# A four-layer convolutional block on one core: earlier loads into the expert layer, a later gate check and fewer PSUM turns

## The chip, the cores and the metric

The kernel runs on one core of one Trainium2 chip. All data are 32-bit floats. The metric is the device time of one execution, in microseconds (us); "before" below is the median of three executions. PE is the matrix engine, DVE the vector engine, ACT the scalar engine, POOL the GpSimd engine, and SP the engine that does little but issue transfers.

## The reference

The input has 8 images of 384 channels and 32 x 32 pixels. Four layers follow one another, each as a residual on a group norm of 32 groups:

```python
x = x + attention(_gn(x))   # layer 0: q, k, v = pw @ gelu(bn(depthwise3x3(x))); softmax(q k) v per head
                            #          (8 heads); w_out; bn over the batch
x = x + experts(_gn(x))     # layer 1: 4 experts, w2 @ relu(w1 @ x + b1) + b2, summed with coefficients
x = x + conv7(_gn(x))       # layer 2: depthwise 7x7, reflected edges
x = x + branches(_gn(x))    # layer 3: three branches; gelu(mw1 x) mw2 on two quarters of the channels,
                            #          depthwise kxk on the others (k = 1, 3, 5), fused with weights
                            #          that come from the branches' means; final projection
```

In layer 1 the gate gives each token its two best experts. The coefficient of an expert depends on whether the expert is chosen by any token at all in first place, and in second place (`present`). Since all four are normally chosen in both places, the kernel computes the coefficients as if that were so, checks afterwards that it was, and computes layers 1 to 3 again if not. That branch isn't taken with these inputs.

## The kernel before, in words

**Order and buffers.** PE, ACT and DVE keep the order in which the program issues their instructions (`manual_schedule(engines=ORDERED)`); in layers 2 and 3 POOL does too. SP issues only transfers, in one queue[...]. Buffers come from pools. A tile of a pool opened with `reuse_waits="tile"` waits only for the last users of the very memory that it overlaps; in other pools the first use waits for everything that lay in the pool's memory before.

**Layer 0.** Depthwise convolutions are matmuls with band matrices (L467). Projections of q and k (L613) and v (L668), scores (L715), exponentials on ACT (L722), values (L734) and the output projection (L790) follow; its result z goes to DRAM from POOL's queue. While the last image is computed, x of each image is read again for statistics (SP).

**From layer 0 to layer 1.** The batch norm of z gives a scale `zn_s` and a shift `zn_t` (`bn_coefs`; the power -1/2 is on POOL). The group norm of layer 1 is worked out from moments of z and x without a pass over their sum: a chain of small DVE operations, a matmul that sums over the groups (gn_ps, L264), `from_moments`, with the powers on POOL (s, L290). `experts()` then opens its pools. `residual(b)` loads z and x in three parts each (L1096, L1097) and adds them on DVE (L1103) to r; `normed` makes xn from r on ACT.

**Layer 1.** For each image b and half h, `TODO` runs over 12 pairs of expert and third of the hidden channels: matmuls ph (L1267), relu on ACT. DVE forms sums of the hidden tiles (`HSUMS`, L1161), POOL has formed sums of weights (`WSUMS`, L1147, 13 operations), and the products p (L1168) of these are added to r on DVE (L1182, L1184). While image b + 1 runs, the generator `next_layer(b)` (called `passing` in the loop) takes image b on to layer 2: statistics, group norm, then for each third of the channels ACT xn (`pass_on`), a transpose on DVE (L957) and a store. The loop calls it after the hidden tiles k = 0, 2, 3, 4, 6 and 8. `logits(b)` (called `gating`) computes the gate, for the last image also the check: ranks of the experts per token, whether any token chose each (anyp), a matmul with ones (pp, L1028), and the flag `repeat`.

**Layer 2.** `convolve7` (L1045) runs over groups of channels. xt are the transposed images, loaded by SP (L1583) for the second and third group. Weights w come through `load_weights` (L1450), are combined at two edges on POOL, and spread by ACT (wx, L1471). Finished groups are evicted from PSUM by ACT (o, L352).

**Layer 3.** `convolve3` (L1716) works as layer 2 does. Two PSUM buffers of four banks each take turns:

```python
def four_banks(turn=True):
    ps = tps[len(taken) % 2].tile([P, 4, HF], FP, tag="ps", name="ps")
    if turn:
        taken.append(1)
    return ps
```

`banks(turn)` cuts small pieces from such a buffer. With `turn=False` the next caller gets the same buffer. A group of convolutions is 160 matmuls, and after the first 80 of some groups `hidden3(i)` (L1916) computes the hidden channels of two images in a buffer of its own. `branch_mean` (L1948), `branch_weights` (L1971) and the bias pb (L1824) are small matmuls in such buffers too. A POOL queue of transfers reorders y in DRAM meanwhile (ya<-y), and SP loads it. The final projection (L2128) follows.

Of the kernel before, what the change touches and what calls it, by code (L numbers as in the profile page):

```python
# [18 lines left out]
P = 128  # L19
# [117 lines left out]
def conv_mixer_kernel(ctx: ExitStack, tc: tile.TileContext, a: dict, out: bass.AP):  # L137
# [13 lines left out]

    parity = const.tile([P, 2], FP, name="parity")
# [122 lines left out]
    def from_moments(own, ps, ref, s, t, gm, firsts=None):  # L275

        c, n = ps.shape[1], ps.shape[3]
        both, sq = (
            own.tile([P, c, n], FP, tag=f"fm_{k}", name=f"fm_{k}") for k in "ab"
        )  # L280
        nc.vector.tensor_copy(both, ps[:, :, 0])
        nc.vector.tensor_mul(sq, both, both)
        nc.vector.scalar_tensor_tensor(
            out=sq, in0=ps[:, :, 1], scalar=EPS, in1=sq, op0=ALU.add, op1=ALU.subtract
        )
        nc.vector.tensor_add(gm, both, ref)
        for n0, n1 in firsts or ((0, n),):
            shape = [P, c, n1 - n0]
            half = mhalf[:, 0:1].unsqueeze(2).to_broadcast(shape)
            nc.gpsimd.tensor_tensor(  # L290
                out=s[:, :, n0:n1], in0=sq[:, :, n0:n1], in1=half, op=ALU.pow
            )
            nc.vector.scalar_tensor_tensor(
                out=t[:, :, n0:n1], in0=gm[:, :, n0:n1], scalar=-1.0, in1=s[:, :, n0:n1],
                op0=ALU.mult, op1=ALU.mult,
            )
# [13 lines left out]
    def bn_coefs(stats, gb, n, s, t):  # L310

        mv = small.tile([P, 2, 9], FP, tag="bn_mv", name="bn_mv")
        for i in range(n):
            nc.vector.bn_aggr(mv[:, :, i], stats[:, i].rearrange("p a s -> p (a s)"))
        rsqrt(s, mv[:, 1, :n])
        nc.vector.tensor_mul(s, s, gb[:, :, 0])
        nc.vector.tensor_mul(t, mv[:, 0, :n], s)
        nc.vector.tensor_sub(t, gb[:, :, 1], t)
# [18 lines left out]
    mv3 = const.tile([P, 2, NC, B], FP, name="mv3")  # L337

# [19 lines left out]
    with (  # L358
# [6 lines left out]
        bn_gb = load(cw, "bn_gb", nc.scalar)  # L365
        stats = cw.tile([P, 9, 2 * B, 6], FP, name="stats")
# [11 lines left out]
        with tc.tile_pool(name="cgn", bufs=2, space=PSUM) as cgn:  # L378
            for b in range(B):
                nc.sync.dma_start(out=x0[:, b], in_=a["x"][b, :, 0])  # L380
                nc.sync.dma_start(out=x1[:, b], in_=a["x"][b, :, 1])
                x_stats(0, b, x0[:, b])
                x_stats(1, b, x1[:, b])
            norms = {0: gn_coefs((mvx[:, 0, :2], mvx[:, 1, :2]), cgn)}
# [142 lines left out]
    def layers(again, early, xst, pre_pool, pp0, pw):  # L527
        s1, t1, gm1 = (early.tile([P, NC, B], FP, name=f"{n}1") for n in ("s", "t", "gm"))
        gmy = early.tile([P, NC, 2], FP, name="gmy")
        zpool = ExitStack()  # L530
        zs = zpool.enter_context(tc.tile_pool(name="zs", bufs=1))
# [5 lines left out]
        b2s = load(zs, "b2")  # L537
        consts = zs.tile([P, NC, 2], FP, name="consts")
        nc.gpsimd.tensor_copy(consts[:, :, 0], bn_gbo[:, :, 1])
        for i in (0, 2):  # L540
            nc.gpsimd.tensor_tensor(
                out=b2s[:, :, i], in0=b2s[:, :, i], in1=b2s[:, :, i + 1], op=ALU.add
            )
        nc.gpsimd.tensor_tensor(out=consts[:, :, 1], in0=b2s[:, :, 0], in1=b2s[:, :, 2], op=ALU.add)

        def attention(shifted):
# [3 lines left out]
            with tc.tile_pool(name="aw", reuse_waits="tile", bufs=1) as aw, tc.tile_pool(  # L550
# [32 lines left out]
                chk = aw.tile([P, B * 2 * NP], FP, name="chk")  # L583
# [319 lines left out]
        bn_coefs(zst, bn_gbo, NC, zn_s, zn_t)  # L903
        with tc.tile_pool(name="mg", bufs=1, space=PSUM) as mg:
            shape = [P, NC, B]
            pm = mg.tile([P, NC, 2], FP, tag="gmy", name="pm")
            over_groups(pm, consts, range(NC))
            nc.vector.tensor_copy(gmy, pm)
            mz, vz, dz, dx, cv, mr, vr = (
                zs.tile(shape, FP, tag=f"mom{i}", name=f"mom{i}") for i in range(7)  # L910
            )

# [7 lines left out]
            v = nc.vector  # L920
            for o, q in ((dz, mvz), (dx, mvxh)):
                v.tensor_sub(o, *by_half(q[:, 0]))
# [3 lines left out]

            v.tensor_mul(dx, dx, dz)
            v.tensor_scalar(dx, dx, 0.5, None, ALU.mult)
            v.scalar_tensor_tensor(out=cv, in0=cv, scalar=2.0 / N, in1=dx, op0=ALU.mult, op1=ALU.add)
            v.tensor_mul(dz, dz, dz)  # L930
            v.scalar_tensor_tensor(out=vz, in0=dz, scalar=0.5, in1=vz, op0=ALU.mult, op1=ALU.add)
            v.tensor_mul(mr, mz, by_channel(zn_s))
            v.scalar_tensor_tensor(out=mr, in0=mr, scalar=0.5, in1=mvx[:, 0], op0=ALU.mult, op1=ALU.add)
            v.tensor_add(mr, mr, by_channel(zn_t))
            v.tensor_mul(vr, vz, by_channel(zn_s))
            v.scalar_tensor_tensor(out=vr, in0=vr, scalar=0.5, in1=cv, op0=ALU.mult, op1=ALU.add)
            v.tensor_mul(vr, vr, by_channel(zn_s))
            v.tensor_add(vr, vr, mvx[:, 1])
            ref = zs.tile(shape, FP, name="ref")
            dq = zs.tile([P, NC, 2, B], FP, name="dq")  # L940
            v.tensor_add(ref, gmx, gmy[:, :, 0:1].to_broadcast(shape))
            centred(dq, mr, vr, ref)
            ps = mg.tile([P, NC, 2, B], FP, tag="gn", name="gn_ps")
            over_groups(ps, dq, range(NC))
            from_moments(zs, ps, ref, s1, t1, gm1, ((0, 1), (1, B)))
        zpool.close()
        pre_pool.close()

# [72 lines left out]
        def any_chosen(at, gtile, ones, pool):  # L1021
            anyp = gtile("anyp", [2, E])
            for k in range(2):
                nc.vector.tensor_reduce(
                    anyp[:, k], at[:, k].rearrange("p t e -> p e t"), AX.X, ALU.max
                )
            pp = pool.tile([P, 2 * E], FP, tag="sm", name="pp")
            nc.tensor.matmul(pp, lhsT=ones, rhs=anyp.rearrange("p k e -> p (k e)"), start=True, stop=True)  # L1028
            present = gtile("present", [2, E])
            nc.vector.tensor_scalar(present.rearrange("p k e -> p (k e)"), pp, 0.5, None, ALU.is_gt)  # L1030
            return present
# [39 lines left out]
        def experts():  # L1071
# [6 lines left out]
            ew = ewpool.enter_context(tc.tile_pool(name="ew", bufs=1))  # L1078
# [10 lines left out]

            def residual(b):  # L1090
                r = rs[b] = er.tile([P, NC, N], FP, tag="r", name="r")
                vs = []
# [9 lines left out]
                for ct in range(NC):  # L1102
                    nc.vector.scalar_tensor_tensor(  # L1103
                        out=r[:, ct, :], in0=r[:, ct, :], scalar=zn_s[:, ct : ct + 1], in1=vs[ct],
                        op0=ALU.mult, op1=ALU.add,
                    )
# [3 lines left out]

            def normed(b, h):
                xn = xns[b, h] = wq.tile([P, NC, HF], FP, tag="xn", name="xn", bufs=2)
# [6 lines left out]
            first = residual(0)  # L1119
            next(first)  # L1120
            w1 = wq.tile([P, E, NC, HID], FP, tag="w1", name="w1")
            b1 = load(ew, "b1")
            for e in range(E):
                nc.sync.dma_start(out=w1[:, e], in_=a["w1"][:, e])
            w2 = load(ew, "w2")
            b2 = load(ew, "b2")
            gate_w, gate_b = load(ew, "gate_w"), load(ew, "gate_b")
            badd = ew.tile([P, NC], FP, name="badd")
            tb1 = ew.tile([P, NC, B], FP, name="tb1")
            ref2 = er.tile([P, NC, B], FP, tag="ref2", name="ref2", bufs=1)  # L1130
            ones = ew.tile([P, P], FP, name="ones")
# [9 lines left out]
            nc.vector.tensor_mul(tb1, s1, zn_t.unsqueeze(2).to_broadcast([P, NC, B]))  # L1141
            nc.vector.tensor_add(tb1, tb1, t1)
            next(first)
            normed(0, 0)
            nc.gpsimd.memset(ones, 1.0)
# [57 lines left out]
            def norm2(ps, b, cos, st):  # L1203
                c = slice(cos[0], cos[-1] + 1)
                from_moments(er, ps[:, c], ref2[:, c, b : b + 1], *(st[:, c, i : i + 1] for i in range(3)))
# [23 lines left out]
            def logits(b):  # L1229
# [17 lines left out]
                if b < B - 1:  # L1247
                    return

                def gtile(name, shape):  # L1250
                    return ew.tile([P, *shape], FP, tag=name, name=name)

                present = any_chosen(chosen(lg, gtile), gtile, ones, eh)
                least = gtile("least", [1])
                nc.vector.tensor_reduce(least, present.rearrange("p k e -> p (k e)"), AX.X, ALU.min)
                nc.vector.tensor_mul(least[:1], least[:1], bounded)
                nc.vector.tensor_scalar(repeat, least[:1], 0.5, None, ALU.is_lt)
                yield

            ahead, passing = None, None  # L1260
            for b, h in product(range(B), range(2)):
                hs = ew.tile([P, NC, E, HF], FP, tag="hs", name="hs")
                gating = logits(b)
                for k, (e, dc) in enumerate(TODO):
# [7 lines left out]
                    if h == 0 and passing and k in (0, 2, 3, 4, 6, 8):  # L1272
                        next(passing)
# [18 lines left out]
            return passing  # L1292


        def experts_by_token():


            with tc.tile_pool(name="gw", bufs=1) as gw, tc.tile_pool(
# [6 lines left out]
                nc.gpsimd.memset(ones, 1.0)  # L1305
                lg = gw.tile([P, NT, E], FP, name="lg")
# [60 lines left out]
                present = any_chosen(at, gtile, ones, gh)  # L1367
# [111 lines left out]
        with tc.manual_schedule(engines=ORDERED | {mybir.EngineType.Pool}):  # L1479
            if again:  # L1480
                last = iter(())
            else:
                last = experts()
            ewpool.close()
# [23 lines left out]
            for c in range(2):  # L1508
# [3 lines left out]
                for _ in range(4 if c == 0 else B):  # L1512
                    next(last, None)
            for c, e in product(range(2), repeat=2):
                convolve7(ps0, 0, c, e, begun.pop((c, e)), slice(HB, B))
                if (c, e) != (1, 1):
                    next_weights()
        erpool.close()
# [218 lines left out]
        with tc.manual_schedule(engines=ORDERED | {mybir.EngineType.Pool}):  # L1737

            for ct in range(NC):
                o = None  # L1740
                for c in range(8):
# [25 lines left out]
                    if ct == 0 and c == 4:  # L1767
                        load3()
                    if ct == 2 and c == 5:
# [52 lines left out]
            pb = banks().tile([MR, B])  # L1822
# [80 lines left out]
            def hidden3(i):  # L1903


                slot, units = banks(), []
# [34 lines left out]
            def branch_mean():  # L1941
# [3 lines left out]
                slot = banks()  # L1945
# [145 lines left out]
            def first():  # L2091
                wms[0] = weights3(0, banks())
# [224 lines left out]
```

## Time and profile before

| what | value |
|---|---|
| median of three executions | 3262.89 us (3262.3 to 3269.65) |
| profiled execution, its own time | 3265.67 us |
| its span, first to last instruction | 3263.7 us |
| mean granted clock of PE | 0.974 |
| PE busy (matmul) | 3046.0 us, 93% |
| DVE busy | 1694.3 us, 52% |
| ACT busy | 1186.5 us, 36% |
| POOL busy | 264.5 us, 8% |
| transfers | 322.83 MB, mean 99 GB/s |

All positions below are microseconds from the span's start. A line of the timeline gives start, duration, engine, source line, operation, output and inputs, shape and count, and in brackets how long the engine was idle before, with the instruction that ended it. A line of the chain of waits gives start, duration and what was waited for or executed. A line of the windows gives the stretch, its length, the busy time of PE, PE's weight loads, DVE, ACT and POOL, the granted clock, the busy share of the 16 DMA engines and the rate.

### The profile page before, as it was taken

Reading aid. Unit: us, or ns where it says so; the run is one execution under the profiler, and the core shown is the slowest. Engines: PE = TensorE matmul, PEld = TensorE weight load, DVE = VectorE, ACT = ScalarE, POOL = GpSimd, SP = SyncE. Lnnn points to the kernel's source line nnn. Section 1 sums busy time; section 2 is a strip of 40 time slices with the busy share of each in tenths; the row PEclk is TensorE's granted clock in tenths of the full one; section 3 lists DMA queues with packets and bytes.
Section 4 is the critical chain, followed back from the end, with each engine's and each line's share of the span. In section 5 each row is a group of like instructions: output and inputs, shape, how many; then the busy total and the mean of one; then the engine's idle time right before and its main releaser. Section 6 shows DMA issues by size and latency. Waiting matters only on the chain.

```text
span 3263.7 us, 42215 instructions
## 1 busy us (share of the span) xinstructions
PE 3046.0 (93%) x17740; PEld 1606.7 (49%) x17740; DVE 1694.3 (52%) x2566; ACT 1186.5 (36%) x1340; POOL 264.5 (8%) x415
## 2 busy tenths in 40 slices
PE   5997999999999999999996999999999988986899
PEld 4774333343434333333432665666656656555443
DVE  6997354444454444444442555555546544465064
ACT  3644443535353544535341112122122122445420
POOL 3332000000000000000002000000000000111300
PEclk9999999999999999999997999999999999988899
DMA  6887011020111011110013022022022105867566
GB/s 220 290 282 263 22 43 57 22 80 22 61 42 61 22 58 44 39 61 22 32 35 126 20 62 77 24 75 68 22 79 62 25 25 175 298 190 256 178 215 199
DMA packets 88176, 322.83 MB, mean 99 GB/s; under 512 B 13464, under 2 KB 15856, under 8 KB 83752
## 3 DMA queue, kind: packets, MB, share of 16 engines
q1 hardware_dynamic: 64312, 251.72, 22.6%
q10 hardware_dynamic: 13488, 35.81, 3.4%
q0 software_dynamic: 10176, 32.51, 3.0%
q8 instruction: 141, 2.31, 0.3%
q14 instruction: 59, 0.48, 0.0%
HBM read 211.66 MB, written 111.68 MB: 99 GB/s over the span
## 4 chain that ended last, share of the span: by engine, by line
PE 72%; DVE 11%; DMA 7%; issue 6%; ACT 3%; POOL 1%; ACTq 0%; SPq 0%; DVEq 0%; POOLq 0%
PE av L734 13%; PE sc L715 13%; PE p L1168 11%; PE ph L1267 11%; PE sc L613 7%; PE sc L668 4%; PE sc L790 3%; DVE hs_sum L1161 2%; DMA w<-in_w 2%; DVE stats L210 2%; DVE y L436 2%; PE ps L1716 2%; PE ps L1045 1%; DMA r<-r 1%; DMA x<-x 1%
## 5 line engine op out<-in xcount | busy, mean ns | idle before, releaser
L722 ACT ACTIVATE e<-sc 128x1024 f32<-128x1024 f32 x512 | 483.0, 1029 | 544.2 <-PE sc L715 543.9
L1267 PE MATMUL ph<-xn,w 128*128 128x512 f32 x1152 | 508.1, 599 | 20.6 <-ACT xn L308 20.6
L715 PE MATMUL sc<-qT,kT 64*128 64x512 f32 x2048 | 477.6, 603 | 10.4 <-ACT e L722 10.4
L734 PE MATMUL av<-e,vT 128*64 128x512 f32 x2048 | 467.7, 598 | 0.0
L1271 ACT ACTIVATE hs<-ph,b 128x512 f32<-128x512 f32 x192 | 132.0, 687 | 744.5 <-PE ph L1267 744.5
L1267 PEld LDWEIGHTS ph<-xn,w 128*128 128x128 f32 x1152 | 218.7, 192 | 284.9 <-issue 256.2
L715 PEld LDWEIGHTS sc<-qT,kT 64*128 64x128 f32 x2048 | 185.6, 186 | 297.5 <-issue 228.7
L734 PEld LDWEIGHTS av<-e,vT 128*64 128x64 f32 x2048 | 135.5, 136 | 316.5 <-issue 316.5
L613 PE MATMUL sc<-y,pw 128*128 128x512 f32 x576 | 251.2, 597 | 8.8 <-ACT y L308 8.8
L467 PE MATMUL ps<-xt,wx 64*64 64x256 f32 x3456 | 196.7, 386 | 39.3 <-DVE xt L403 21.9
L1182 DVE TENSOR_TENSOR r<-r,p 128x256 f32<-128x256 f32 x416 | 157.0, 416 | 127.1 <-PE p L1168 126.4
L750 DVE LOAD_MASK_SELECT sm<-av x64 | 0.9, 14 | 423.9 <-PE av L734 423.9
L752 DVE RECIPROCAL inv<-sm 128x512 f32<-128x512 f32 x64 | 214.6, 3353 | 2.2
L467 PEld LDWEIGHTS ps<-xt,wx 64*64 64x64 f32 x3456 | 158.9, 137 | 76.1 <-issue 38.6
L1045 PE MATMUL ps<-xt,wx 64*64 64x256 f32 (+1 forms) x2912 | 163.8, 384 | 23.2 <-ACT wx L1471 13.5
L613 PEld LDWEIGHTS sc<-y,pw 128*128 128x128 f32 x576 | 109.5, 191 | 150.1 <-issue 138.0
L1168 PE MATMUL p<-hs_sum,wsum 128*128 128x256 f32 x768 | 173.6, 379 | 0.0
L1168 PEld LDWEIGHTS p<-hs_sum,wsum 128*128 128x128 f32 x768 | 145.9, 190 | 19.8
L1161 DVE TENSOR_TENSOR hs_sum<-hs,hs_sum 128x768 f32<-128x768 f32 (+1 forms) x192 | 147.3, 781 | 5.0
L1045 PEld LDWEIGHTS ps<-xt,wx 64*64 64x64 f32 x2912 | 107.9, 142 | 77.6 <-ACT wx L1471 15.3
L668 PE MATMUL sc<-pw_v,y 128*128 128x384 f32 x384 | 127.5, 493 | 5.2 <-ACT y L308 5.2
L352 ACT COPY o<-ps 128x2048 f32<-128x2048 f32 x56 | 103.8, 1855 | 74.7 <-PE ps L467 30.6
(319 smaller groups left out, 3269.9 us busy)
## 6 DMA issues: line engine op xcount, KB each, us to landing
raw<-y SPq DMA_DIRECT2D x72, 512.0 KB
y<-raw SPq DMA_DIRECT2D x24, 1536.0 KB
x<-x SPq DMA_DIRECT2D x23, 608.0 KB
xt<-x SPq DMA_DIRECT2D x23, 608.0 KB
w<-in_w ACTq DMA_DIRECT2D x36, 384.0 KB
xn<-in_x SPq DMA_DIRECT2D x24, 512.0 KB
x<-in_x SPq DMA_DIRECT2D x16, 768.0 KB
z<-z POOLq DMA_DIRECT2D x16, 768.0 KB, 4.3
```

Source lines behind the costliest of these rows:

```text
L467: nc.tensor.matmul(ps[64 * d : 64 * d + 64, 2 * i + e, cc], lhsT=w[r, 12 * cc + 6 * e + 3 * d + k, :], rhs=xt0s[ct][r, 16 * d + 4 * u + 2 ...
L613: nc.tensor.matmul(ps[:, h, :], lhsT=w[:, ct, pair, :], rhs=y[:, ct, h * HF : (h + 1) * HF], start=ct == 0, stop=ct == NC - 1,)
L668: nc.tensor.matmul(ps[:, m, :C], lhsT=y[:, ct, (m0 + m) * P : (m0 + m + 1) * P], rhs=pw_v[:, ct, :], start=ct == 0, stop=ct == NC - 1,)
L715: nc.tensor.matmul(sc[:, s, :], lhsT=kTs[b][r, pair, m * P : (m + 1) * P], rhs=qTs[b][r, pair, h * HF : (h + 1) * HF], start=True, stop=True,)
L722: nc.scalar.activation(e, sc, AF.Exp, scale=1.0 if shifted else HD**-0.5)
L734: nc.tensor.matmul(av[64 * s : 64 * s + 64, :], lhsT=vTs[0][:, m, c0 : c0 + 64], rhs=e[:, s, :], start=m == 0, stop=m == N // P - 1,)
L752: nc.vector.reciprocal(inv, sm)
L1045: nc.tensor.matmul(ps[64 * d : 64 * d + 64, 2 * i + e, c % 2, images], lhsT=w[r, d * K7 + k, :], rhs=by_slot(xts[ct])[r, 16 * d + column(c ...
L1161: nc.vector.tensor_add(rows_of(o, hs, s), rows_of(i, hs, s), rows_of(j, hs, s))
L1168: nc.tensor.matmul(ps[:, :QF], lhsT=block(w)[:, e], rhs=rows_of(x, hs, e), start=e == 0, stop=e == E - 1,)
L1182: nc.vector.tensor_tensor(out=o, in0=o, in1=ps[:, :QF], op=op)
L1267: nc.tensor.matmul(ph, lhsT=w1[:, e, ct, dc * P : (dc + 1) * P], rhs=xns[b, h][:, ct, :], start=ct == 0, stop=ct == NC - 1,)
```

## The change

It has four parts, named A to D below.

A. The constants that `middle` needs are loaded and summed over the groups at the start of layer 0 (`consts`, `gmy`). The pool `zs` becomes part of `early`, and `pre_pool` is closed right after the attention, so that the expert layer's tiles r and x lie over memory that the attention frees early, and w1 over memory freed with them; `ew` waits by tile; xn has four buffers. The first image's r and x are loaded and added in halves of the pixels (`by_halves`). The norm chain is ordered anew: what doesn't need `zn_s` goes ahead of it, the first-half additions lie behind the group sum, scale and shift of image 0 come first, and those of the other images after xn of the first half is under way. The memset of a tile of ones on POOL is gone from `experts`.

B. `passing` is called after k = 0, 2, 3, 4, 5 and 6.

C. `logits` no longer holds the check. `check_gates` forms `any_at` in layer 2, when the last image has been passed on; a small matmul and the flag follow in `decide` later in layer 2. `experts` becomes a generator that is continued in layer 2, so that the pool `ew` lives on there.

D. pb, `hidden3(1)` to `hidden3(3)`, `branch_mean` and the first `weights3` take no turn of the PSUM buffers.

The core of the diff:

```diff
+        bn_gbo, b2s = (load(cw, k, nc.scalar) for k in ("bn_gbo", "b2"))
+        consts = cw.tile([P, NC, 2], FP, name="consts")
...
+            pm = cgn.tile([P, NC, 2], FP, tag="gmy", name="pm", bufs=1)
+            over_groups(pm, consts, range(NC))
+            nc.scalar.copy(gmy, pm)
...
-        zpool = ExitStack()
-        zs = zpool.enter_context(tc.tile_pool(name="zs", bufs=1))
+        zs = early
...
             attention(again)
-        bn_coefs(zst, bn_gbo, NC, zn_s, zn_t)
-        with tc.tile_pool(name="mg", bufs=1, space=PSUM) as mg:
+        pre_pool.close()
+
+        def middle(pool, tag):
...
+            coefs = bn_steps(zst, bn_gbo, NC, zn_s, zn_t)
+            next(coefs)
...
+            next(coefs, None)
...
-            from_moments(zs, ps, ref, s1, t1, gm1, ((0, 1), (1, B)))
-        zpool.close()
-        pre_pool.close()
+            yield
+            rest = from_moments(zs, ps, ref, s1, t1, gm1, 1)
+            next(rest)
+            yield
+            next(rest, None)
+            yield
...
-            ew = ewpool.enter_context(tc.tile_pool(name="ew", bufs=1))
+            ew = ewpool.enter_context(tc.tile_pool(name="ew", bufs=1, reuse_waits="tile"))
...
+            def by_halves(b):
+                begin_residual(b)
+                for h in range(2):
+                    cols = slice(h * HF, (h + 1) * HF)
+                    nc.sync.dma_start(out=rs[b][:, :, cols], in_=zraw[b][:, :, cols])
+                    v, v2 = (wq.tile([P, N], FP, tag="xr", name="xr", bufs=2) for _ in range(2))
+                    v = v.rearrange("p (c n) -> p c n", n=HF)
+                    nc.sync.dma_start(out=v, in_=a["x"][b, :, :2, cols])
+                    nc.sync.dma_start(out=v2[:, :HF], in_=a["x"][b, :, 2, cols])
+                    yield
+                    for ct in range(NC):
+                        add_x(b, ct, cols, v[:, ct] if ct < 2 else v2[:, :HF])
+                yield
...
-                xn = xns[b, h] = wq.tile([P, NC, HF], FP, tag="xn", name="xn", bufs=2)
+                xn = xns[b, h] = wq.tile([P, NC, HF], FP, tag="xn", name="xn", bufs=4)
...
+            norm1 = middle(eh, "sm")
+            next(norm1)
+            next(first)
+            next(norm1)
+            shifts(0, 1)
+            normed(0, 0)
+            w2, b2 = load(ew, "w2"), load(ew, "b2")
+            next(first)
+            next(norm1)
+            shifts(1, B)
...
-            nc.gpsimd.memset(ones, 1.0)
...
-                    if h == 0 and passing and k in (0, 2, 3, 4, 6, 8):
+                    if h == 0 and passing and k in (0, 2, 3, 4, 5, 6):
                         next(passing)
...
-                present = any_chosen(chosen(lg, gtile), gtile, ones, eh)
-                least = gtile("least", [1])
...
+            for _ in passing:
+                yield
+            check_gates(lg, ew.tile([P, NC, E, HF], FP, tag="hs", name="hs")[:, 0, :2].rearrange("p e n -> p (e n)"))
+            yield
...
+        def decide(pp):
+            least = small.tile([1, 1], FP, tag="least", name="least", bufs=1)
+            present = presence(any_at, small.tile([1, 2, E], FP, tag="gates", name="gates", bufs=1), pp, one)
...
-                for _ in range(4 if c == 0 else B):
+                for _ in range((4, 5)[c]):
                     next(last, None)
...
+            next(last, None)
+        ewpool.close()
         erpool.close()
...
                     if ct == 0 and c == 4:
                         load3()
+                        if not again:
+                            decide(banks(False).tile([1, 2 * E]))
...
-            pb = banks().tile([MR, B])
+            pb = banks(False).tile([MR, B])
...
-                slot, units = banks(), []
+                slot, units = banks(i == 0), []
...
-                slot = banks()
+                slot = banks(False)
                 pa = slot.tile([P, 2, B])
...
-                wms[0] = weights3(0, banks())
+                wms[0] = weights3(0, banks(False))
```

## The prediction

> **What bounds the kernel now.** I read first the chain's shares and the slices, then the chain in detail around the attention's end, then PE's waits and timeline in the three other places that the diff touches, then the windows there.
>
> ```profile
> PE   5997999999999999999996999999999988986899
> PEclk9999999999999999999997999999999999988899
> PE 72%; DVE 11%; DMA 7%; issue 6%; ACT 3%; POOL 1%; ACTq 0%; SPq 0%; DVEq 0%; POOLq 0%
> ```
>
> PE is 93% busy and holds 72% of the chain: most of the span can't be shortened by a reordering. What can go are PE's gaps: slice 22 (1714 to 1795) and the slices from 36 on, where the clock drops too. The chain from 1700 to 1790 (start, duration, what):
>
> ```profile
> 1733.20 7.49 DMA z<-z
> ...
> 1741.40 0.20 POOL ones L1145
> 1741.60 0.86 POOL zn_s L205
> ...
> 1744.86 3.18 PE gn_ps L264 x14
> ...
> 1748.76 4.50 POOL s L290 x2
> ...
> 1753.28 3.69 DMA r<-z
> ...
> 1758.31 10.95 DMA xr<-in_x
> ...
> 1769.35 2.17 DVE r L1103
> ...
> 1771.55 0.82 ACT xn L308
> ...
> 1772.42 17.73 PE ph L1267 x37
> ```
>
> The attention's last matmul is at 1732.3, the first expert matmuls run from 1772.4: norm chain, then loads of r and x, one after another. PE's timeline at the other places:
>
> ```profile
> 2643.02 1.99 PE L1168 MATMUL p<-hs,wsum 128*128 128x256 f32 x8 [2.08 <-DVE r L1184]
> 2686.12 0.57 PE L1028 MATMUL pp<-anyp,ones 128*128 128x8 f32 x2 [9.12 <-DVE anyp L1024]
> 2769.22 6.09 PE L1045 MATMUL ps<-xt,wx 64*64 64x256 f32 x80 [3.64 <-ACT wx L1471]
> 2998.28 8.43 PE L1916 MATMUL ps<-y,mw1s 128*72 128x512 f32 x16 [5.18 <-ACT xt L352]
> 3018.19 4.62 PE L1716 MATMUL ps<-xt,wx 64*64 64x256 f32 x80
> 3026.27 7.25 PE L1716 MATMUL ps<-xt,wx 64*64 64x256 f32 x80 [3.45 <-ACT o L352]
> 3048.59 6.26 PE L1716 MATMUL ps<-xt,wx 64*64 64x256 f32 x80 [3.50 <-ACT o L352]
> 3069.92 5.93 PE L1716 MATMUL ps<-xt,wx 64*64 64x256 f32 x80 [3.50 <-ACT o L352]
> ```
>
> The same 80 convolution matmuls take 4.62 us undisturbed and 7.25, 6.26, 5.93 us after an idle. The windows (PE, weight load, DVE, ACT, POOL, clock, DMA share, GB/s) say why, and what else is busy:
>
> ```profile
> 3025.00:3035.00 10.00, 8.73 (x84) 4.76 (x85) 0.00 (x0) 3.24 (x5) 0.00 (x0) 0.66 0.19 62
> 3045.00:3055.00 10.00, 6.50 (x85) 4.07 (x82) 0.00 (x0) 4.13 (x7) 6.70 (x14) 0.83 0.90 297
> 3055.00:3065.00 10.00, 10.00 (x76) 4.23 (x78) 0.00 (x0) 3.62 (x10) 9.19 (x20) 1.00 0.85 268
> ```
>
> [...] granted 0.66 after the 3.45 us idle, 1.00 in undisturbed windows. So an idle of 3.5 us costs more than its length. [...] the power zn_s, whose input the DVE had at 1738.05, runs at 1741.57, just after the memset `ones` queued ahead of it. [...] the 0.90 share at 297 GB/s in 3045 to 3055 is what compression of that stage has to reckon with.
>
> **A, attention to experts.** Moved: the first half of r and x and w1 go behind the attention's last x load (about 1690), since their memory is freed then; on SP two half loads of x, four of w1 and one of r are ahead of b1, the gate weights, r half 1 and x half 1. Their bytes, 2.36 MB (w1) + 0.79 + 0.79, need 13 us at the 297 GB/s above, with 42 us to 1732. They pass the z writes, which POOL issues. Removed: the memset. Moved to the start: the constants' group sum (PE pm 3.12 us), in a stretch (13.5 to 31.8 us) where PE is idle; cost 0. My chain after: DVE ve 1738.05; pow 0.89 to 1738.95; 16 dependent DVE operations of about 0.12 to 1741.0; gn_ps 3.18 to 1744.2 (three half additions of about 0.7 on DVE beside it); four fm operations 0.6; pow of three columns about 0.9 to 1745.8; t and tb 0.7; ACT xn 0.85; PE at 1747.4. Gain 25.0, less 1.7 for the four expert matmuls that before ran at 1759.31: **23.3 us**, bounds 18 and 26. The 21-column pow (about 3.6 of the 4.50) is behind the first xn. Late next: w2, issued about 1744.5, which took 10.7 before (issue 1754.61, first sum 1765.27), then 13 POOL sums of 1.26: to 1771.6. The first products come 30.9 after PE's start (1772.42 to 1803.28 before), at 1778.3: 6.7 us of cover, thin. DVE waits with x half 1 for its load, but nothing needs DVE before those products.
>
> **B, the next layer's steps at k = 4, 5, 6 in place of 4, 6, 8** (seven images). xn and the transposed x alternate in two buffers, so the third ACT xn waits for the second transpose (DVE, 2623.49 to 2625.48); the relu behind it, due at 2623.77, runs 3 us late; with two ph buffers PE loses about 1.3. But PE waits 2.08 at 2643.02 for a DVE chain that starts after the third transpose, which its own x<-x load gates and which doesn't move: the loss falls into that wait. **0 us**; bounds +9 (1.3 x 7 unabsorbed) and -5.
>
> **C, the gate check.** Removed from PE's path: 9.12 idle + 0.57 for pp: **9.6 us**. Put instead on DVE in layer 2 after the last transposes (from about 2757, some 9 us; DVE is idle there until about 2800), and a matmul and four tiny DVE operations later. Behind it on SP wait the second group's xt loads, about 2766 in place of 2762, needed at about 2803. Of the layer-2 weights two loads are no longer made at 310 us but queue behind seven xt loads: 5.35 MB, 16 to 21 us with spreading, against 27 us to the first convolution: 0. And SP's second x<-x, ready 2757.4, was issued at 2762.10, after a weight load's slot; ACT's o eviction (2766.18) waited for it, and PE idled 3.64. With the check's order it follows the first directly. **2.5 us**, bounds 0 and 3.6.
>
> **D, PSUM turns.** Two four-bank buffers alternate. A hidden3 in the middle of a group takes the other buffer and a turn, so the next group gets the first one back and waits for its eviction. With no turn taken, that group goes into the buffer hidden3 used, long read. Saved: 3.45 + 2.63 (7.25 - 4.62) = 6.1; 3.50 + 1.64 = 5.1; 3.50 + 1.31 = 4.8; hidden3(0): its inputs were ready at 2993.9, it took 8.43 against 7.09: 5.7 (4.4 + 1.3); branch_weights' wait of 3.51 (3085.53): 3.2 at most. Sum 24.9. The stage's transfers (reorder, y, weights) must come 24 us faster in total: I take **22 us**, bounds 10 and 26. The final projection starts after the last convolution and moves with it.
>
> At the start, four small loads leave the path behind 308: 0.5 us, 0 to 2.
>
> **Sum**: 23.3 + 0 + 9.6 + 2.5 + 22 + 0.5 = 57.9. The profiled execution took 3265.7 (span 3263.7); 3265.7 - 57.9 = 3207.8; the median 3262.9 lies 2.8 lower, so **3205 us**.
>
> **Rivals.** (1) In D the DMA engines become the bound (0.90 and 0.85 shares speak for it, 0.19 in 3025 to 3035 against): weights or reordered y come late, D gives 10: 3217. (2) A's loads don't come early: r, x or w1 still wait for the attention's end because some overlapped tile is released late, or w2's sums delay the first products: A gives 11: 3217. Were the memory claim simply void, only memset and reordering count (about 5.5 us): 3223. (3) B is not absorbed: 3214. (4) **Slower**: B's third xn holds ACT, behind it all relus. To lose more than 58 + 10 us over seven images, each must lose 9.7 us on PE; with 2.1 of wait and 1.7 of buffer to swallow, relus would be 13.5 late, which needs the second transpose 10 us later than now: its x<-x load (under 3.6 us of DVE wait) would have to take 13, as xr's 10.95 did at 1758. Then 3272 and up. Nothing in 2600 to 2645 points to it.
>
> **Numbers.** Sum as worked out 0.58 (3190 to 3213); rival 1 0.14, 2 0.13, 3 0.08; two of them together 3229 or 3223. Slower 0.04 (rival 4, and a layer-2 load late by tens of us), no change 0.03. Within 0.3%, about 10 us, this kernel's measurement can't be told from no change. Range 3190 (all upper bounds: 26 + 5 + 13.2 + 26 + 2 = 72) to 3232 (two rivals at once).
>
> **What would show it.** First expert matmul about 15 us after the attention's last, not 40; no POOL memset; r and x off the chain there. No pp before the last expert half of layer 1. Eviction waits of 3.5 gone at hidden3, and all 80-matmul groups near 4.62 with a clock of 1.00. Wrong: a wait of PE on DMA or POOL at the first products; waits "<-ACT wx" or "<-DMA y" in layer 3; PE idle at ph on ACT with xn ahead.

## The result and the profile after

The kernel after takes 3208.93 us (median of four, 3205.7 to 3219.3); before took 3264.27 in the same series (four executions, 3262.3 to 3269.65). The ratio is 0.9833 with a 95% interval of 0.9807 to 0.9859: faster by 1.4 to 1.9%. Forecast were 3205 us, 3190 to 3232. The profiled execution of after has a span of 3205.5 us, 58.2 less than before's 3263.7.

The slices and the chain's shares on the page of after:

```profile
PE   4988999999999999999998999999999999886999
PEclk9999999999999999999998999999999999988999
PE 74%; DVE 13%; DMA 6%; issue 4%; ACT 2%; POOL 1%; SPq 0%; ACTq 0%; DVEq 0%; POOLq 0%
```

PE's share of the chain is up from 72 to 74%, slice 22 from a 6 to an 8; the chain has more DVE and less DMA: what is left between the attention and the experts is the norm chain, not loads. In that stretch the chain of waits of after reads:

```profile
1741.48 0.94 POOL zn_s L207
...
1744.95 3.15 PE gn_ps L266 x14
...
1748.85 0.84 POOL s L294
...
1750.25 0.82 ACT xn L314
1751.12 33.26 PE ph L1302 x72
```

No memset, no r<-z, no xr<-in_x. PE's timeline of after at the other places (a second convolution group of 80 runs on from the first, so a line counts 160):

```profile
2611.10 7.99 PE L1302 MATMUL ph<-xn,w 128*128 128x512 f32 x18 [1.77 <-ACT hs L1306]
2626.30 1.99 PE L1213 MATMUL p<-hs,wsum 128*128 128x256 f32 x8 [0.30 <-DVE r L1229]
2736.67 9.45 PE L1061 MATMUL ps<-xt,wx 64*64 64x256 f32 x168 [2.50 <-ACT wx L1535]
2960.88 7.09 PE L1981 MATMUL ps<-y,mw1s 128*72 128x512 f32 x16 [0.53 <-DVE mw1s L1975]
2979.45 9.00 PE L1779 MATMUL ps<-xt,wx 64*64 64x256 f32 x160
2995.40 9.00 PE L1779 MATMUL ps<-xt,wx 64*64 64x256 f32 x160
3011.34 9.00 PE L1779 MATMUL ps<-xt,wx 64*64 64x256 f32 x160
3031.42 12.44 PE L1779 MATMUL ps<-xt,wx 64*64 64x256 f32 x192 [2.80 <-ACT o L365]
```

The three waits of 3.5 us for an eviction (ACT's copy of a finished group out of PSUM) are gone, and 160 matmuls take 9.00 us: 4.5 for 80, at a granted clock of 1.00 throughout. Cut into stages at the same instructions of both traces, with the prediction's sums beside them (the attention's last matmul is the small one that starts at 1732.21 in before):

| stage, from and to | before | after | difference | predicted |
|---|---|---|---|---|
| start to the attention's last matmul | 1732.21 | 1735.59 | +3.4 | -0.5 |
| to the first products (A) | 71.07 | 48.62 | -22.5 | -23.3 |
| to the first matmul of layer 2 (B, C) | 930.56 | 921.23 | -9.3 | -9.6 |
| to the matmuls behind layer 2's first eviction (C) | 35.38 | 31.23 | -4.2 | -2.5 |
| to the end (D) | 494.48 | 468.83 | -25.7 | -22.0 |
| sum | 3263.70 | 3205.50 | -58.2 | -57.9 |

The sum agrees better than its parts. Two errors, a loss of 3.4 at the start where a gain was expected and 5.3 us too little for D and the eviction, cancel each other. So the 57.9 against 58.2 is in part luck.

### The profile page after: what moved, and what is told of

It is laid out like the page before. It is cut to its first block, busy times and chain, and to the rows that moved or that the text cites. A ratio compares the mean times of both kernels' runs of the same rounds, so it can differ in the third digit from the quotient of the medians.

```text
span 3205.5 us, 42222 instructions
## 1 busy us (share of the span) xinstructions
PE 3030.8 (95%) x17740; PEld 1601.8 (50%) x17740; DVE 1692.7 (53%) x2570; ACT 1186.8 (37%) x1341; POOL 262.7 (8%) x415
## 4 chain that ended last, share of the span: by engine, by line
PE 74%; DVE 13%; DMA 6%; issue 4%; ACT 2%; POOL 1%; SPq 0%; ACTq 0%; DVEq 0%; POOLq 0%
PE av L748 14%; PE sc L729 14%; PE p L1213 11%; PE ph L1302 11%; PE sc L627 7%; PE sc L682 4%; PE sc L804 4%; DVE stats L212 3%; DVE y L460 2%; DVE hs_sum L1206 2%; DMA x<-x 1%; PE ps L1779 1%; PE po L2193 1%; PE po L2196 1%; PE po L2204 1%
## 5 line engine op out<-in xcount | busy, mean ns | idle before, releaser
L1061 PEld LDWEIGHTS ps<-xt,wx 64*64 64x64 f32 x2912 | 111.0, 138 | 67.8 <-ACT wx L1535 15.5
```

The lines of the kernel that those rows point to most:

```text
L1061: nc.tensor.matmul(ps[64 * d : 64 * d + 64, 2 * i + e, c % 2, images], lhsT=w[r, d * K7 + k, :], rhs=by_slot(xts[ct])[r, 16 * d + column(c ...
```

## The experiments

Stages below are cut as in the table. Medians are compared with before as run in the same series (3268 to 3271 us there).

**D alone, and D taken back.** `turns_alone` is before with the four edits of part D, `turns_undone` is after without them:

```diff
-            pb = banks().tile([MR, B])
+            pb = banks(False).tile([MR, B])
-                slot, units = banks(), []
+                slot, units = banks(i == 0), []
-                slot = banks()
+                slot = banks(False)
-                wms[0] = weights3(0, banks())
+                wms[0] = weights3(0, banks(False))
```

> The kernel before with part D alone (the small matmuls keep the PSUM turn). If the turns are worth what the two traces show and the parts add up, 25.0 us faster than before (3264.3 to about 3239), with no PE wait for an eviction at the convolutions of layer 3's second unit but one, and 80 matmuls in 4.62 or less after each hidden3. Rival, that the transfers of layer 3 become the bound when the rest of the kernel isn't changed: 10 us faster, with PE waits on wx or y between 2998 and 3090.

> The kernel after with part D alone taken back. If additive: 25.0 us slower than after (3208.9 to about 3234); the three waits of 3.5 us for an eviction come back, each with a clock below 1.00 behind it. If instead parts A and C had let layer 3's transfers run earlier and so made D's gain possible or needless, the loss differs from 25 by more than 5 us.

Measured: 3241.75 us for D alone (ratio to before 0.9921, 0.9906 to 0.9937), 3236.19 for after without D (0.9904, 0.9888 to 0.9919). From layer 2's first matmul to the end D alone takes 502.4 us where before takes 529.9, and after without D takes 526.5 where after takes 500.1: 27.5 gained, 26.4 lost. The waits in the timeline of after without D:

```profile
2967.65 9.36 PE L1981 MATMUL ps<-y,mw1s 128*72 128x512 f32 x16 [5.57 <-ACT xt L365]
2996.56 6.04 PE L1779 MATMUL ps<-xt,wx 64*64 64x256 f32 x80 [3.45 <-ACT o L365]
3017.67 7.40 PE L1779 MATMUL ps<-xt,wx 64*64 64x256 f32 x80 [3.50 <-ACT o L365]
3040.14 6.26 PE L1779 MATMUL ps<-xt,wx 64*64 64x256 f32 x80 [3.50 <-ACT o L365]
```

and in that of D alone:

```profile
2995.48 7.09 PE L1916 MATMUL ps<-y,mw1s 128*72 128x512 f32 x16 [0.53 <-DVE mw1s L1910]
3014.05 9.00 PE L1716 MATMUL ps<-xt,wx 64*64 64x256 f32 x160
```

The same waits, of the same length, come and go with these four edits whatever stands around them. D is shown to be worth 26 to 27 us, and nothing in A to C makes or spoils it. The idle is 3.5 each time; the 80 matmuls behind it take 6.0 to 7.4 where 4.5 is undisturbed, and which of the three pays most differs from one kernel to the other. The granted clock of after without D says why (windows in the prediction's form):

```profile
2996.14:2999.56 3.42, 3.00 (x28) 1.79 (x32) 0.00 (x0) 0.37 (x1) 0.00 (x0) 0.50 0.05 16
3016.62:3023.45 6.83, 5.78 (x56) 3.44 (x60) 0.00 (x0) 2.02 (x3) 4.96 (x11) 0.50 0.87 296
3040.52:3043.93 3.41, 3.41 (x40) 2.14 (x36) 0.00 (x0) 0.00 (x0) 0.48 (x1) 0.50 0.60 216
```

It is 0.50 for 3.41, 6.83 and 3.41 us. PE works for 3.00, 5.78 and 3.41 us of these at 0.50, which by the clock alone costs 1.5, 2.9 and 1.7 us; measured over 4.5 are 1.5, 2.9 and 1.8. So what an idle of 3.5 us cost here went with how long PE worked at 0.50 behind it. Why one of the three stretches is twice as long as the others was not shown.

The rival that the transfers become the bound falls with the windows of after (length; PE, weight load, DVE, ACT, POOL busy; clock, DMA share, GB/s):

```profile
2995.00:3005.00 10.00, 10.00 (x164) 6.30 (x163) 0.31 (x1) 7.58 (x15) 5.64 (x12) 1.00 0.91 320
3004.00:3014.00 10.00, 10.00 (x72) 4.08 (x68) 0.00 (x0) 3.54 (x10) 7.71 (x16) 1.00 0.87 273
```

DMA is busy 0.91 at 320 GB/s, and PE all the time at a clock of 1.00: the transfers are dense, but PE doesn't wait for them.

**The gate check left out of before.**

```diff
-                if b < B - 1:
-                    return
...
-                present = any_chosen(chosen(lg, gtile), gtile, ones, eh)
...
-                nc.vector.tensor_scalar(repeat, least[:1], 0.5, None, ALU.is_lt)
-                yield
+                if b == B - 1:
+                    nc.gpsimd.memset(repeat, 0)
```

> The kernel before without the gate check (the flag for a repeat is a constant 0, so the ranks of the experts and whether any token chose each aren't computed). If the check's cost on PE's path is its 9.12 us of idle and 0.57 us of matmul: 9.6 us faster than before, about 3254.7, with layer 2 starting 9.3 to 9.7 us earlier than 2733.84. Rival, that the wait would only move to the next hidden tile's relu or to DVE's sums: under 4 us. Nothing in layer 2 is reordered here, so the first eviction of layer 2 should still come late (2766 less the shift) and PE should idle about 3.6 us for it: a larger gain than 9.7 in layer 2's start would be chance of the clock.

Measured: 3259.35 us, ratio 0.9973 (0.9965 to 0.9982); from the first products to layer 2 920.58 us, 10.0 less than before and 0.7 less than after. In its timeline the expert matmuls go through where the wait was:

```profile
2674.61 0.38 PE L1244 MATMUL pt<-ident,lt 128*128 128x128 f32 x2
2674.83 23.34 PE L1257 MATMUL ph<-xn,w 128*128 128x512 f32 x54
```

So the check costs its wait and its matmul, and nothing takes its place. Layer 2's first eviction stays late, 30.6 us behind layer 2's start (32.3 in before, 28.2 in after), and PE idles 4.62 for it.

**The constants back to where they were.** `consts_late` is after with b2 loaded and summed in `layers()` as in before, and the group sum's matmul at the head of `middle`:

```diff
-        bn_gbo, b2s = (load(cw, k, nc.scalar) for k in ("bn_gbo", "b2"))
...
-            pm = cgn.tile([P, NC, 2], FP, tag="gmy", name="pm", bufs=1)
-            over_groups(pm, consts, range(NC))
-            nc.scalar.copy(gmy, pm)
...
+        b2s = load(zs, "b2")
...
+            pm = pool.tile([P, NC, 2], FP, tag=tag, name="pm")
+            over_groups(pm, consts, range(NC))
+            nc.scalar.copy(gmy, pm)
             coefs = bn_steps(zst, bn_gbo, NC, zn_s, zn_t)
```

It takes two small loads off ACT's queue at the start. The load in question is SP's sixteenth of x, issued at 23.87 in after and at 19.74 in before.

> The kernel after with the constants taken back to where they were loaded before (b2 with the attention's constants, the group sum's matmul in the gap behind the attention's last matmul). Theory: [...] SP issues it at 23.87 in place of 19.74 and everything behind is 2.1 us late, later 3.4; then the first convolution is back at 50.65 (52.61 in after), the attention ends 2 to 3.4 us earlier than 1735.78, and the time is 2 to 3.4 us below after. Rival, that PE's queue is to blame (the group sum waits for POOL's consts until 25.0, and gn_ps queues behind it until 28.02): the same gain, but the sixteenth load would still be issued at 23.9 and the last statistics start at 27.75. Third case: the matmul back in the gap costs as much as it saves (PE is idle there for 9.2 us, so not expected): no difference.

Measured: the first convolution at 50.68, as in before (50.65; 52.61 in after). SP's timeline shows the last of the sixteen loads of x, first in after, then in before, then in this kernel:

```profile
23.87 0.33 SPq L405 DMA_DIRECT2D o<-in_x  x1
```

```profile
19.74 0.33 SPq L381 DMA_DIRECT2D o<-in_x  x1
```

```profile
19.88 0.33 SPq L394 DMA_DIRECT2D o<-in_x  x1
```

and the chain of waits of after says what it waited for:

```profile
19.99 3.86 DMA bn_gb<-in_bn_gb
23.87 3.85 DMA o<-in_x
```

bn_gb is a 9 KB load on ACT's queue, which itself starts at 19.99, when gmem is stored (12.80 to 19.83 in the same chain). SP's waits name it in both kernels, first in after, where the sixteenth load of x waits for it, then in before, where it is a load of xn behind that one:

```profile
SPq L405 <- DMA bn_gb<-in_bn_gb: 5.5, 1, 5.5
```

```profile
SPq L431 <- DMA bn_gb<-in_bn_gb: 4.0, 1, 4.0
```

So with two more small loads on ACT's queue the wait for bn_gb falls on the sixteenth load of x, and without them that load is issued at 19.88 again. Why a load on SP's queue waits for one on ACT's was not shown. The rival, PE's queue, falls: it would have left the load at 23.9, and in after the group sum is out of gn_ps's way by 28.02, and the statistics that gn_ps needs come at 29.3.

The median, 3209.62 us (0.9819, 0.9806 to 0.9832), shows no gain over after. Of the 1.9 us, 0.9 is left at the attention's end (1734.72) and nothing at layer 2's start. The stages between differ from one profile to the next by as much: 17.5 to 18.8 us for the projection of v, 33.1 to 33.7 from the experts to the products, 228 to 232 from layer 0's first convolution to the first projection, all with the same instructions.

**Loads of r and x held back.** Three tiny memsets on DVE behind dq make the first-half loads wait:

```diff
+            norm1 = middle(eh, "sm")
+            next(norm1)
             first = by_halves(0)
             next(first)
...
+                    if h == 0:
+                        nc.vector.memset(v[:, :, :1], 0.0)
+                        nc.vector.memset(v2[:, :1], 0.0)
+                        nc.vector.memset(rs[b][:, :, :1], 0.0)
+                    nc.sync.dma_start(out=rs[b][:, :, cols], in_=zraw[b][:, :, cols])
```

> The kernel after, but the first half of image 0's r and x (not w1) may only be loaded when DVE has finished dq of the norm chain (three tiny memsets of those tiles behind dq, about 1745). Theory: 1.57 MB are then issued at about 1745 and land at about 1751; additions 2.1, then the rest of the norm chain 2.2 and xn 0.9: the expert matmuls start 20.5 us after the attention's last matmul in place of 15.5, and 5 us are lost. So early loads are worth 5 of the 22.5 us of part A, and the other 17 come from loads that no longer follow one another behind the norm chain, from the memset and from the order of the chain. Rival, that the early loads carry most of part A: 12 us or more are lost. Second rival, that they are worth nothing since the norm chain hides them: under 1 us.

Measured: 3214.53 us (ratio 0.983, 0.9815 to 0.9845), and 20.65 us from the attention's last matmul to the experts, 5.1 more than after. Its chain:

```profile
1747.19 5.64 DMA xr<-in_x
...
1752.96 2.08 DVE r L1111 x3
```

So the early start of these loads is worth 5 us by itself: the other 17 us of A are had even if they start at 1746.6. In before's chain these loads come one after another, r (3.69) behind the norm's power of 4.50, the third part of x (10.95) behind the first addition (lines in the prediction); here they take 6.3 us together. That this, the shorter power and the missing memset make up the 17 us is read from the two chains; no run shows their shares.

**Two xn buffers, and `ew` waiting as before.** Each is one word:

```diff
-                xn = xns[b, h] = wq.tile([P, NC, HF], FP, tag="xn", name="xn", bufs=4)
+                xn = xns[b, h] = wq.tile([P, NC, HF], FP, tag="xn", name="xn", bufs=2)
```

```diff
-            ew = ewpool.enter_context(tc.tile_pool(name="ew", bufs=1, reuse_waits="tile"))
+            ew = ewpool.enter_context(tc.tile_pool(name="ew", bufs=1))
```

> The kernel after with two xn buffers in place of four, so that w1 lies partly over the attention's last weights and its loads may wait for the attention's last matmul (1735.6) as before. Theory: 2.36 MB are needed only at 1751 (and a quarter of them then), so even if issued at 1735.6 they land by 1744: under 1 us. Rival, that loads of r queue behind the waiting w1 on SP and come late: 3 us or more, with PE waiting for xn behind a DVE wait for r<-z. If w1 is loaded as early as in after, the edit doesn't do what it says and nothing follows.

> The kernel after with the pool ew waiting as before for all that lay in its memory, not tile by tile. Theory: b1, the gate weights and tb1 then wait for the attention's last z transfer (about 1744), and SP holds r and x of the second half behind them, but all of these are needed only from 1750 on: under 1 us, 15.5 to 16.5 us from the attention's last matmul to the experts. Rival: the wait for the transfer, 7.5 us in before, comes back in the chain (tb ahead of xn): 3 us or more.

Measured: with two xn buffers w1 does wait for the attention's last weights (first lines of SP's timeline behind 1696, in that kernel):

```profile
1736.23 0.80 SPq L1159 DMA_DIRECT2D w<-in_w  x2
1737.15 0.54 SPq L1137 DMA_DIRECT2D r<-z  x1
```

and the load of r behind it on SP's queue is issued at 1737.15 (1696.69 in after), yet the experts still start 15.53 us behind the attention, as in after; 3211.28 us (0.9822, 0.9807 to 0.9837). With `ew` waiting as a whole it is 15.78 us; 3207.73 us (0.9817, 0.9802 to 0.9832). Taken singly, neither the early w1 nor the tile-wise waits of `ew` carry part A. What the removed memset and the new order of the norm chain are worth, one by one, wasn't tried.

**B taken back.**

```diff
-                    if h == 0 and passing and k in (0, 2, 3, 4, 5, 6):
+                    if h == 0 and passing and k in (0, 2, 3, 4, 6, 8):
```

> The kernel after with part B taken back (the next layer's steps after k = 4, 6, 8). Theory: the 7 waits of PE for relu (8.2 us in all) go, the 7 waits for the residual on DVE grow from 4.3 to about 12 us, and the time from the first products to layer 2 changes by less than 1 us. Rival, that part B itself costs the 8.2 us: layer 2 starts 8 us earlier. Rival, that B gains: layer 2 starts later by several us.

Measured: PE's waits in layer 1 (total, times, longest), first in after, then with B taken back:

```profile
PE ph L1302 <- ACT hs L1306: 8.2, 7, 1.8
PE p L1213 <- DVE r L1229: 4.3, 7, 0.7
```

```profile
PE p L1213 <- DVE r L1229: 12.4, 7, 2.5
```

8.2 us of new waits stand against 8.1 us less of the old one. From the experts' start to layer 2 it is 953.0 us without B, 954.3 and 954.6 in two profiles of after: B costs some 1.5 us, a little more than the 1 us allowed; the median (3209.42) shows nothing. The other traces agree: 953.4 to 956.4 us in the eight traces that have A, B and C, 953.0 and 952.6 in the two with A and C alone, some 2 us on average.

**One more turn fewer.** `best` is `consts_late` with one further edit:

```diff
-                pg = banks().tile([P, NC, 3, B])
+                pg = banks(False).tile([P, NC, 3, B])
```

> The kernel after with two edits: the constants as in consts_late (first convolution 1.9 us earlier), and branch_weights takes no PSUM turn either, so that the next group goes into its buffer and waits for a DVE read (done 0.3 us after its last matmul) in place of the eviction. Theory: PE's 2.80 us wait at the first group of layer 3's last unit goes, 2.5 us are gained there, and with the constants about 4 us against after: some 3205 us where after gives 3209, if the clock's phases don't take it back. Rival: the turns of the later groups swap and the next eviction is waited for instead, nothing is gained at the end of the fusion.

Measured: 3209.64 us (0.9817, 0.9803 to 0.983), no gain. The wait at the fusion is gone and has moved one group on:

```profile
3027.82 10.79 PE L1779 MATMUL ps<-xt,wx 64*64 64x256 f32 x192 [0.32 <-DVE wb L2042]
3038.60 2.17 PE L2098 MATMUL ps<-cbias,proj 128*128 128x8 f32 x18
3047.87 9.52 PE L1779 MATMUL ps<-xt,wx 64*64 64x256 f32 x144 [7.10 <-ACT o L365]
```

The bias's matmuls (L2098) between the two groups take a turn, so the later group now gets the buffer of the group just finished and waits 7.10 for its eviction; in after it waits 1.76. The rival was right: turns have to be counted over the whole sequence.

**Constants and B both taken back.** `both_back` is `consts_late` with B taken back too, run beside after:

> The kernel after, unchanged, beside the two others: 3209 us, and stages as in its first profile within about 1.5 us each. Stages that differ between the two profiles of the same program (the first products, 33.1 us; the projection of v, 38.9 and 17.5) show what a difference of one profile is worth.

> The kernel after with the constants as in consts_late and the passing steps as in passing_468. Theory: the first convolution 1.9 us earlier, and 1.4 us less from the start of the experts to layer 2 (954.3 in after, 953.0 in passing_468): about 3.3 us below after_again, if these add up and clock phases don't take them. Rival: the whole is set elsewhere and no difference from after_again can be seen (under 1 us).

Measured: after 3209.22 us (3207.82 to 3211.17, five runs), `both_back` 3203.07 (3202.28 to 3208.9, five runs; ratio to before 0.9808, 0.9795 to 0.9822). The two ranges overlap by a microsecond; the medians differ by 6.2, and 3.3 were expected. By the medians it is the fastest version run here. Its trace has the first convolution 2.1 us earlier and 2.0 us less from the experts to layer 2 than this profile of after, 4.1 of the 5.6 by which the spans differ (3200.4 against 3206.0); the rest is spread over stages with the same instructions.

## Why the prediction was right, and where it wasn't

**Bound and range.** PE's gaps were what could go, and they went where they were named. The time lies 4 us above the forecast and inside the range.

**A, right.** The steps held to 0.6 us each: the power started 5.9 us behind the attention's last matmul (5.8 predicted), gn_ps 9.4 (8.8), ph 15.5 (15.2). The 16 dependent DVE operations took 2.4 us in place of 2.0. The thin cover over w2 was enough: loaded in 10.8 us (10.7), POOL's sums ended at 1775, the first products started at 1784. What the prediction left open, how much hangs on the early loads alone, is 5 us.

**The start, wrong.** "Cost 0" for the moved constants and "0.5, 0 to 2" for fewer loads were the failed step. The working counted PE's matmul and looked whether PE was idle; it did not count that with two more loads on ACT's queue a later load on SP's queue is issued at 23.87 in place of 19.74. That costs 2.0 us at the first convolution: it starts at 52.4 to 52.8 in the seven traces with the constants moved, at 50.5 to 51.6 in the six with them where they were. The attention's end scatters more, 1733.7 to 1738.9 in the seven and 1732.2 to 1734.7 in the six, 1736.2 and 1733.4 on average. So some 2.8 of the 3.4 us go with the edit, and before's own profile was early by about a microsecond. Whether and why the loss at the attention's end is larger than 2.0 stays open.

**B, right in kind.** PE stalls of 1.17 us (1.3 predicted) fell into the wait at the products, which shrank from 12.0 to 4.3 us in all. B left 1.5 to 2 us, which the estimate of 0 didn't have.

**C, right on the check:** 10.0 us where it alone is left out, 9.6 predicted. The 9.3 of the table is what C gains there less what B costs: with B taken back the same stage takes 919.3 us, 11.3 less than before.

**C, right on the eviction's mechanism, under-sized in its worth.** SP's waits for the x<-x stores of the last image (in total, times, longest), in before and then in after, and the eviction in the kernel without the check, which keeps the old order:

```profile
SPq L983 <- DMA w<-in_w: 8.4, 1, 8.4
```

```profile
SPq L999 <- DVE x L973: 16.4, 2, 9.5
SPq L999 <- POOL x L975: 1.3, 2, 0.8
```

```profile
2755.87 1.86 ACT L352 COPY o<-ps 128x2048 f32<-128x2048 f32 x1 [8.62 <-DMA x<-x]
```

In before the second store waits for a weight load that ACT's queue issued at 2754.27 and that in the chain takes 7.75 us, to 2762.03; the store is issued at 2762.10, 4.7 us after its data are ready (2757.4). In after it waits for its data alone, as the prediction said. It is issued 26.5 to 28.3 us behind layer 2's start in the three traces with the old order and 23.7 to 25.3 in the ten with the new one, and the eviction follows at 30.6 to 32.4 and at 27.3 to 28.3. The gain of 4.2 us (32.3 to 28.2) lies above the 2.5 and above the bound of 3.6. The timeline of after names a load of projb as what ended ACT's wait, but that load was issued 0.4 us behind the second store, and in the program the eviction waits for both stores and not for that load.

**D, right, and discounted for nothing.** Measured piece by piece in the two traces: hidden3(0) 6.0 (5.7 predicted), the three groups 6.3, 5.4 and 5.0 (6.1, 5.1, 4.8), the branch weights 1.8 (at most 3.2): 24.6 against 24.9, of which 3 were taken off for transfers that then kept up. The last piece gave little, since the first group of the next unit now waits 2.80 for the eviction, which the prediction didn't foresee. The matmuls that ran slow behind the idles of before carried some 7.3 us of D's worth, three tenths of it (8.43 where 7.09 is undisturbed, and 7.25, 6.26 and 5.93 where 4.5 is). In the runs the clock was 0.50 behind each of the three idles without D and 1.00 in these groups with it.

**Rivals.** DMA as the bound, late loads and the unabsorbed B are each contradicted by a view above. The slower case had no trace: the relu behind the third xn is late by one short wait, not by 13 us.

## What to carry to other kernels

Where two buffers alternate, count who takes a turn over the whole sequence of groups: one small matmul between two large ones can make each group wait for the eviction of the last, and taking away one turn can move the wait to a dearer place. A wait is worth its length plus the slow matmuls behind it, here 3.5 us and another 1.4 to 2.9. A transfer moved to an idle time is not free: in this program two small loads more on ACT's queue had a 512 KB load on SP's queue issued 4.1 us later.

## What the runs showed that was not expected

- Transfers on SP's queue waited for loads on ACT's: two loads of 3 and 6 KB on ACT's queue moved the issue of a 512 KB load on SP's queue from 19.74 to 23.87, and a weight load held a store whose data were ready by 4.7 us.
- Of part A's 22.5 us, loading r and x 50 us earlier carries only 5.1.
- The same idle of 3.5 us cost 1.4 to 2.9 us of slow matmuls: 5.93 to 7.40 for 80 that take 4.5 at a clock of 1.00; in `turns_undone` PE worked at 0.50 for 3.00, 5.78 and 3.41 us behind it and lost 1.5, 2.9 and 1.8.
- The clock fell behind a shorter idle too: in before PE was busy for 1.07 of the 3.41 us up to 2745.02, its longest idle 2.34 (before layer 2's gn_ps), and the clock was 0.50 from 2745.02 to 2751.84.
- Stages with the same instructions differ by 1 to 4 us between profiles (layer 0's convolutions to the first projection 228 to 232, the experts to the first products 32.9 to 34.0), so an effect below some 2 us is seen only at its own place, not in a time.
